# Row-max placings moved from GpSimd's DMA queue to SyncE's, with held-back stack fills and new transfer costs in the planner of an attention and FFN kernel

## Chip, cores and metric

The kernel runs on one core of one Trainium2 chip. The metric is the device time of one execution in microseconds (us), lower is better. Before the change it is 1095.73 us, the median of 3 runs (1094.55 to 1102.3).

## What is computed

One transformer block over x of shape 2 x 1024 x 512, all in float32. With xn the layer norm of x:

```
qkv  = xn @ w_qkv.T + b_qkv                    # 32 heads of 16
s    = softmax(q k.T / 4 + alibi, causal) v    # per head
s    = s @ w_out.T + b_out
h    = silu(oct(xn, w_gate)) * oct(xn, w_up)   # 1360 hidden; the weights cut to -1, 0, 1
out  = x + s * silu(oct(h, w_down))
```

`oct` is a linear map whose weight matrix is put together from eight blocks by the multiplication table of the octonions. The softmax is the exact one: the row maximum is subtracted before the exponential.

## The kernel before

**Attention in units.** Heads are worked on in groups of four, in units `(b, g, qc)`: batch `b`, head group `g` (8 of them), half `qc` of the 1024 queries. There are 32 units. Each needs these pieces:

- *Projections* (`qk_items`, L460): q and k of a pair of head groups, in float32. ScalarE and VectorE put the result into a tile `st` as a rounded high part and the remainder, and one transfer of 512 KB on SyncE's queue (L495) sends it to a scratch `sp` in DRAM. The weights of the next pair (`wqr`) are fetched on SyncE's queue (L486) and compacted by GpSimd (`compact_wq`, L151).
- *Stack fills* (`fill_k`, L513, and `fill_q`, L526): the parts are read back from `sp` into stacks `k_stack` (a ring of five) and `q_stack` (a ring of four), four transfers of 128 KB for each, and a fifth of 16 KB with the alibi rows for a k stack. A fill overwrites a stack that an earlier group used, so it waits for TensorE to be done with that one.
- *Maxima* (`max_items`, L537): first score products (L552), `s1` in the program, whose rows VectorE reduces to their maxima (`left`, `mx`). `split_max` (L601) splits the maxima into two float32r parts.
- *Placing* (`place_max`, L611): four transposes on TensorE (L617, tile `pm`), a copy by ScalarE to `mr` (L624), and two transfers of 8 KB (L625 to L628) that put the two parts into rows 126 and 127 of the unit's q stack. They are issued on GpSimd's queue. With these rows the second score product subtracts the row maximum by itself.
- *Exponentials* (`exp_step`, L657): second score products (L668, `s2`), a mask product (L687) on the diagonal, and the exponential by ScalarE from one of two PSUM banks into a tile `p`.
- *Values* (`value_step`, L694): p times v (L706), and `normalise` (L719), whose result goes to a DRAM scratch `att`.

Beside them run side items: v products (L434), the projections of later pairs, the output projection (L775, tiles `ot`, `y`, scratch `proj`), and the preparation of the FFN's weights (three sums `tot_g`, `tot_u`, `tot_d`, and sign expansions that leave through `mw` on GpSimd's queue). After the last unit comes the FFN (L1415 and L1444), in a fixed order.

**What sets the order.** Each engine takes its instructions in the order in which the program wrote them, and SyncE's and GpSimd's queues do so too: a transfer whose wait is not over holds up all that stand behind it. That order is made at build time by a small planner in the kernel (L1097 to L1358). It keeps a clock of TensorE (`now`), and assumed times at which ScalarE, VectorE, PSUM banks and transfers will be done, and always emits the item that is ready first, with priorities. `link` stands for the transfers. An item that needs a placing counts as ready at `placed[u]`, which is 6000 ns after the copy to `mr` (L1207); a fill takes the link for 4500 ns and is there 2500 ns later (L1133, L1134); fetched and stored tiles are there after 6000 and 5000 ns (L1142, L1219); a projection's parts after 4000 ns (L1276). A fill is emitted in `try_fill` (L1122) as soon as its stack is no longer needed by an item still to be emitted. None of these numbers is in the program that runs: there, an instruction waits for the real event, but in the order that the planner chose.

The planner's numbers touch only the stage before the FFN. SyncE's queue has eight completion semaphores in rotation, so its transfers wait in turn for the one eight places before them.

Of the kernel before, what the change touches and what calls it, by code (L numbers as in the profile page):

```python
# [75 lines left out]
def kernel(  # L76
# [21 lines left out]
    act_, dve_, pool_, sp_ = (  # L98
        InOrder(tc, engine, held) for engine in (nc.scalar, nc.vector, nc.gpsimd, nc.sync)
    )  # L100
# [3 lines left out]
    def pe(ins):  # L104

        return tc.keep_in_program_order(ins)
# [301 lines left out]
    def q_of(b, g, half):  # L408
        return q_ring[(2 * (b * NG + g) + half) % 4]
# [201 lines left out]
    def place_max(b, g, qc, tiles):  # L611

        q = q_of(b, g, qc)
        ps = ps_m.tile([P, 512], F32, tag="m", name=f"pm_{b}_{g}_{qc}")
        for tl in range(4):
            pe(
                nc.tensor.transpose(  # L617
                    ps[0:8, tl * P : (tl + 1) * P],
                    tiles["rm"][:, tl].rearrange("p l h -> p (l h)"),
                    ident,  # L620
                )
            )
        mr = wk.tile([8, 512], F32R, tag="mr", name=f"mr_{b}_{g}_{qc}", bufs=1)
        act_.copy(mr, ps[0:8, :])  # L624
        for n in range(2):  # L625
            pool_.dma_start(
                out=q[NR - 2 + n : NR - 1 + n].bitcast(F32),
                in_=mr[4 * n : 4 * n + 4, :].bitcast(F32),  # L628
            )
# [89 lines left out]
    def normalise(b, g, qc):  # L719

        posb = po_tiles.pop((b, g, qc))
        o = op.tile([P, 4, 64], F32, tag="o", name=f"o_{b}_{g}_{qc}")
        pt = ps_m.tile([P, 4, 4, 32], F32, tag="m", name=f"pt_{b}_{g}_{qc}")
        for tl in range(4):
            pe(
                nc.tensor.transpose(
                    pt[:, tl, :, :].rearrange("p h e -> p (h e)"),
                    posb[:, tl * P : (tl + 1) * P],
                    ident,
                )  # L730
            )
        rl = wk.tile([P, 4, 4, 1], F32, tag="rl", name=f"rl_{b}_{g}_{qc}")
        dve_.reciprocal(rl, pt[:, :, :, HD : HD + 1])
        dve_.tensor_tensor(
            o.rearrange("p t (h d) -> p t h d", d=HD),
            pt[:, :, :, 0:HD],
            rl.to_broadcast([P, 4, 4, HD]),
            ALU.mult,
        )
        n = b * (S // P) + 4 * qc  # L740
        sp_.dma_start(
            out=att[n : n + 4, :, g * 64 : (g + 1) * 64].rearrange("t p n -> p t n"), in_=o
        )
# [67 lines left out]
    units = [(b, g, qc) for b in range(B) for g in range(NG) for qc in range(2)]  # L811
# [9 lines left out]
    maxs, mtiles = [], []  # L821
    for u in range(NU):
        its, t = max_items(*units[u])
# [18 lines left out]
    E, V, M = [0], [0], [0]  # L842
    stored = {}
    fills = [0]
    fetches, fetched, last_outs = {}, {}, []
    turned_out = [0]

    def unit_of(lst, n):
        return lst[n][0] if n < len(lst) else NU

    for b in range(B):
        for hh in range(2):
            n = 2 * b + hh
            u = 8 * n
# [10 lines left out]
        for gp in range(2 - 2 * b, NP):  # L865
            n = b * NP + gp
            u = 4 * n
# [6 lines left out]
        for n, qc in enumerate((0, 1) if b + 1 < B else (1, 0)):  # L874
            u = (b + 1) * 2 * NG + n
# [21 lines left out]
    for n in order:  # L897
        if n in seen:
            continue
        k = n  # L900
# [193 lines left out]
    now, kind = [HEAD], ["F"]  # L1094
    act, dve = [0.0], [0.0]
    e_free, x_free, m_free = [0.0] * 2, [0.0] * 3, [0.0] * 2
    o_free = [0.0]  # L1097
    p_ready, placed, fill_at = {}, {}, []
    link = [0.0]
    turns, norms = [], []  # L1100
    S_ = [0]

    def take(pool):
        pool.sort()
        return pool

    def run_pe(k, ready, cost):
        now[0] = max(ready, now[0] + SWITCH.get((kind[0], k), 0)) + cost
        kind[0] = k

    def run_act(t, cost):
        act[0] = max(act[0], t) + cost
        return act[0]

    def run_dve(t, cost):
        dve[0] = max(dve[0], t) + cost
        return dve[0]


    qk_done = [HEAD + 4500]  # L1120

    def try_fill():  # L1122

        n, part = divmod(fills[0], 4)
        if n >= B * NG or len(qk_done) <= (n // 2 + 1 if n > 1 else part // 2):
            return
        if n == 0 and now[0] < qk_done[part // 2] - 4000:
            return
        if unit_of(exps, E[0]) < 2 * (n - 2) + (0, 1, 2, 2)[part]:
            return  # L1130
        (fill_q if part % 2 else fill_k)(n // NG, n % NG, part // 2)
        fills[0] += 1
        link[0] = max(now[0], link[0], qk_done[n // 2 + 1 if n > 1 else part // 2]) + (4500 if n else 3000)  # L1133
        fill_at.append(link[0] + 2500)  # L1134

    def try_fetch():
        for n, k in enumerate(fetches):
            if k in fetched or k not in stored or stored[k] > now[0]:
                continue
            if turned_out[0] == 4 * n:  # L1140
                fetches[k]()
                fetched[k] = now[0] + 6000  # L1142

# [51 lines left out]
    def next_turn():  # L1197
        found = []
        if turns:
            u, t = turns[0]  # L1200

            def go(u=u):
                turns.pop(0)
                place_max(*units[u], mtiles[u])
                run_pe("F", ready, 436)
                take(m_free)[0] = run_act(now[0] + START, 500)
                placed[u] = m_free[0] + 6000  # L1207

            ready = max(t, min(m_free))
            found.append((ready, 1, 0, go))  # L1210
        if norms:
            u, t = norms[0]

            def go(u=u):
                norms.pop(0)
                normalise(*units[u])
                run_pe("F", t2, 436)
                take(m_free)[0] = run_dve(now[0] + START, 600)
                stored[units[u]] = m_free[0] + 5000  # L1219

            t2 = max(t, min(m_free))
            found.append((t2, 2, 0, go))
        return [f for f in found if f[0] < HELD]
# [27 lines left out]
    def next_side(pos):  # L1251
        if S_[0] == len(side):
            return []
        due, ok, (cost, emit, what, *need) = side[S_[0]]
        if not ok():
            return []

        def go():
            emit()
            S_[0] += 1  # L1260
            if cost:
                run_pe("F", ready, cost)
            if what == "none":
                return
            if HELD not in m_free:
                take(m_free)[0] = HELD
            if what is None:
                return
            if what == "v":
                end = run_dve(now[0] + START, 350)  # L1270
            elif what == "qk":
                end = run_dve(run_act(now[0] + START, 600), 700)
                done_qk[0] += 1

                if done_qk[0] % 4 == 0:
                    qk_done.append(end + 4000)  # L1276
            elif what == "t":
                end = run_act(now[0] + START, 500)
            else:
                end = run_dve(now[0] + START, 600)  # L1280
            m_free[m_free.index(HELD)] = end + END

        ready = 0 if HELD in m_free or not cost else min(m_free)
        for k in need:
            ready = max(ready, known[k] + 100)
        return [(ready, 3 if pos >= due else 7, cost, go)]

    def next_behind(pos):
# [62 lines left out]
    while E[0] < len(exps) or V[0] < len(vals) or S_[0] < len(side) or norms or behind:  # L1351
        try_fill()
        try_fetch()
        if not w_again and unit_of(exps, E[0]) >= NU - 5:
            fetch_signs()
        if not step():
            now[0] += 500
            assert now[0] < 1e8  # L1358
# [5 lines left out]
    for t in [  # L1364
# [9 lines left out]
        t = t.rearrange("p h n -> p (h n)")[:, 0 : 12 * P]  # L1374
# [138 lines left out]
    for n, (tb, mt) in enumerate(work):  # L1513
# [10 lines left out]
        if n >= 1 and last_outs:  # L1524
            while True:
                _, emit, kind = last_outs.pop(0)
# [77 lines left out]
```

## Time and profile before

| What | Value |
|---|---|
| median of 3 runs | 1095.73 us (1094.55 to 1102.3) |
| the profiled execution | 1096.36 us, its span 1094.6 us |
| TensorE busy | 1043.3 us (95%) |
| VectorE, ScalarE, GpSimd busy | 676.4, 509.7, 174.4 us |
| transfers on SyncE's queue, and GpSimd's | 98.28 MB, 4.77 MB |
| placings' transfers | 64 of 8 KB, median 2.5 us from issue to landing |
| fills' transfers | 128 of 128 KB for the k stacks, 4.9 us; 128 for the q stacks, 4.4 us |

In the profile PE is TensorE's matmuls, PEld its weight loads, DVE VectorE, ACT ScalarE, POOL GpSimd, SP SyncE; a q behind the name means the engine's queue or sequencer. Tiles are named without their numbers: `q_stack<-mr` is a placing's transfer, `q_stack<-sp` a fill's. All instructions that go through the helper at L69 show that line, so they are told apart by their tiles. Busy shares of PE are of modelled matmul times and overlap a little: a 128x512 product in a row of its like follows the one before by about 0.23 us although each is shown as longer. A float32 product is two instructions in the trace.

### The profile page before, as it was taken

The numbers are of one execution on the slowest core, as the hardware profiler recorded it, in microseconds if no ns is written. First come the engines' busy times: TensorE is split into PE (matmuls) and PEld (weight loads), VectorE is DVE, ScalarE is ACT, GpSimd is POOL, SyncE is SP. The second block draws the span as 40 slices with busy tenths as digits, with TensorE's granted clock in tenths as the row PEclk, the third lists the DMA queues.
The fourth block names the chain that finished last, engine by engine and source line by source line (L and its number), as shares of the span: only waits on it lengthen the run. The fifth ranks groups of instructions, "written<-read, shape, count | busy, mean of one in ns | idle before, by whom it ended". The sixth has DMA issues, their size and how long they took to land. (4 is left out here: it accounts for less than half of the span.)

```text
span 1094.6 us, 15494 instructions
## 1 busy us (share of the span) xinstructions
PE 1043.3 (95%) x5578; PEld 701.0 (64%) x5578; DVE 676.4 (62%) x1405; ACT 509.7 (47%) x958; POOL 174.4 (16%) x290
## 2 busy tenths in 40 slices
PE   9858998999999999999999999999899999999995
PEld 6535565676656566666576665666456678888784
DVE  5358798678878876787887778868432123141312
ACT  3103457675666544555554555566581213232322
POOL 4710003201010011010101000000011123232322
PEclk9979998999999999999999999999999999999998
DMA  5794574445366444384544235841141123030211
GB/s 161 180 162 128 129 141 135 93 83 108 70 165 104 95 107 55 102 165 83 144 71 65 64 65 122 159 84 45 44 131 49 49 58 116 1 116 1 77 39 38
DMA packets 73195, 104.04 MB, mean 95 GB/s; under 512 B 25896, under 2 KB 30640, under 8 KB 73120
## 3 DMA queue, kind: packets, MB, share of 16 engines
q1 hardware_dynamic: 69648, 98.28, 39.5%
q0 software_dynamic: 3472, 4.77, 1.7%
q8 instruction: 45, 0.74, 0.3%
q14 instruction: 30, 0.25, 0.1%
HBM read 69.39 MB, written 33.10 MB: 94 GB/s over the span
## 5 line engine op out<-in xcount | busy, mean ns | idle before, releaser
L69 ACT ACTIVATE p<-s 128x512 f32<-128x512 f32 x576 | 318.6, 595 | 188.6 <-PE s L687 113.0
L668 PE MATMUL s<-q_stack,k_stack 128*128 128x512 f32 (+3 forms) x768 | 255.0, 399 | 4.7 <-ACT p L69 4.3
L552 PE MATMUL s<-k_stack,q_stack 126*128 126x512 f32 (+3 forms) x768 | 238.3, 390 | 7.9 <-DVE mx L69 6.5
L69 DVE TENSOR_REDUCE mx<-s 128x1 f32<-128x384 f32 (+3 forms) x352 | 226.2, 643 | 11.5
L69 DVE TENSOR_REDUCE left<-s 128x1 f32<-128x512 f32 x256 | 164.0, 683 | 38.3 <-PE s L552 37.2
L668 PEld LDWEIGHTS s<-q_stack,k_stack 128*128 128x128 f32 x768 | 134.0, 190 | 74.3 <-ACT p L69 36.1
L552 PEld LDWEIGHTS s<-k_stack,q_stack 126*128 126x128 f32 x768 | 129.2, 191 | 64.2 <-issue 18.4
L69 DVE TENSOR_TENSOR s<-s,mask 128x128 f32<-128x128 f32 (+2 forms) x352 | 123.8, 352 | 47.0 <-PE s L552 46.5
L706 PE MATMUL po<-p,v 128*32 128x512 f32 (+3 forms) x1536 | 140.5, 491 | 0.4 <-ACT p L69 0.4
L476 PE MATMUL pqk<-xnT,wq 128*128 128x512 f32 x256 | 135.5, 629 | 5.0 <-POOL wq L69 4.0
L69 DVE SCALAR_TENSOR_TENSOR h<-pu,sc_u,sg 128x512 f32<-128x512 f32 (+1 forms) x44 | 33.0, 750 | 157.0 <-PE pu L1423 153.7
L69 POOL DMA_DIRECT2D q_stack<-mr x64 | 32.0, 505 | 580.6 <-ACT mr L69 580.6
L69 POOL TENSOR_TENSOR hs<-h,hs 128x512 fp32r<-128x512 f32 (+1 forms) x43 | 56.2, 1306 | 213.0 <-ACT hs L69 213.0
L706 PEld LDWEIGHTS po<-p,v 128*32 128x32 f32 x1536 | 42.8, 109 | 72.9 <-issue 66.1
L687 PE MATMUL s<-mask_r,ident_r 128*128 128x256 f32 (+1 forms) x320 | 89.0, 278 | 0.0
L69 ACT ACTIVATE sg<-pg,sc_g 128x512 f32<-128x512 f32 (+1 forms) x44 | 30.3, 688 | 99.9 <-PE pg L1423 99.8
L476 PEld LDWEIGHTS pqk<-xnT,wq 128*128 128x128 f32 x256 | 47.5, 201 | 31.6 <-issue 21.1
L69 ACT CAST hs<-h 128x512 fp32r<-128x512 f32 (+1 forms) x44 | 27.3, 619 | 85.6 <-DVE h L69 85.6
L434 PE MATMUL pv<-wv,xnT 128*128 128x256 f32 x256 | 66.3, 386 | 0.6 <-ACT md L69 0.6
L687 PEld LDWEIGHTS s<-mask_r,ident_r 128*128 128x128 f32 x320 | 60.5, 189 | 3.1 <-issue 2.2
L775 PE MATMUL pout<-wo_sb,oT 128*128 128x512 f32 x128 | 61.8, 598 | 0.5 <-ACT oT L69 0.5
L434 PEld LDWEIGHTS pv<-wv,xnT 128*128 128x128 f32 x256 | 46.1, 190 | 13.0 <-issue 6.5
(146 smaller groups left out, 1088.9 us busy)
## 6 DMA issues: line engine op xcount, KB each, us to landing
sp<-st SPq DMA_DIRECT2D x32, 512.0 KB, 3.4
k_stack<-sp SPq DMA_DIRECT2D x128, 128.0 KB, 4.9
q_stack<-sp SPq DMA_DIRECT2D x128, 128.0 KB, 4.4
wqr<-in_wqk_dram SPq DMA_DIRECT2D x16, 512.0 KB, 5.2
xt<-in_x_dram SPq DMA_DIRECT2D x16, 256.0 KB, 3.5
att<-o SPq DMA_DIRECT2D x32, 128.0 KB, 3.6
ot<-att SPq DMA_DIRECT2D x16, 256.0 KB, 3.4
proj<-y SPq DMA_DIRECT2D x16, 256.0 KB, 2.0
```

The lines of the kernel that those rows point to most:

```text
L69: ins = issue(*args, **kwargs)
L434: nc.tensor.matmul(ps[:, 0:256], lhsT=xnT[:, c, b * S + kt * P : b * S + (kt + 1) * P], rhs=wv_tiles[2 * b + hh][:, c, :], start=(c == 0), ...
L476: nc.tensor.matmul(ps, lhsT=wq_tiles[b, gp][:, kt, which, :], rhs=xnT[:, kt, b * S + c * 512 : b * S + (c + 1) * 512], start=(kt == 0), st ...
L552: nc.tensor.matmul(ps[:, j * n : (j + 1) * n], lhsT=q_of(b, g, qc)[0 : NR - 2, first + j, tl * P : (tl + 1) * P], rhs=k_of(b, g, c)[0 : NR ...
L668: nc.tensor.matmul(ps[:, c0 : c0 + w], lhsT=k_of(b, g, kt // 4)[0:NR, h, kt % 4 * P : (kt % 4 + 1) * P], rhs=q[0:NR, h, 512 - w : 512], st ...
L687: pe(nc.tensor.matmul(out, lhsT=ident_r, rhs=rhs, start=False, stop=True))
L706: nc.tensor.matmul(po[32 * i : 32 * i + 32, 512 - w : 512], lhsT=v[:, kt, h * VC : h * VC + 32], rhs=p[:, i * part + c0 : i * part + c0 + ...
L775: nc.tensor.matmul(ps, lhsT=turned[t][:, c, :], rhs=wo_sb[0][:, c, :], start=(c == 0), stop=(c == KD - 1),)
```

## The change

Three things are changed, and nothing else. The two transfers of a placing are issued on SyncE's queue instead of GpSimd's. `try_fill` emits no fill while a placing is near, which is when a finished unit's maxima wait for their transposes, when at most five items of a unit's maxima are left, or when a placing has been emitted and its assumed time is not over; the test is left out where the next maxima need just that fill, and for the first group. And every transfer now takes its share of the one `link`: 3400 ns for a k fill and 2700 for a q fill, 1400 for a fetch, 100 for a placing, 700 for a store, 2700 for a projection's parts, each there about 2000 ns later. A placing so counts as there some 2500 ns after its copy instead of 6000. The amount of work on every computing engine stays the same; its order changes in the stage before the FFN.

```diff
@@ place_max
         for n in range(2):
-            pool_.dma_start(
+            sp_.dma_start(
                 out=q[NR - 2 + n : NR - 1 + n].bitcast(F32),
                 in_=mr[4 * n : 4 * n + 4, :].bitcast(F32),
             )
@@ planner
+    def transfer(t, cost):
+
+        link[0] = max(link[0], t) + cost
+        return link[0]
+
+    def placing_soon():
+
+        if M[0] == len(maxs):
+            return False
+        u, n, count, *_ = maxs[M[0]]
+        if fills[0] <= 4 * (u // 2) + 1 + 2 * units[u][2]:
+            return False
+        return bool(turns) or count - n <= 5 or any(p > now[0] for p in placed.values())
+
     def try_fill():
...
+        if n and placing_soon():
+            return
         if unit_of(exps, E[0]) < 2 * (n - 2) + (0, 1, 2, 2)[part]:
             return
         (fill_q if part % 2 else fill_k)(n // NG, n % NG, part // 2)
         fills[0] += 1
-        link[0] = max(now[0], link[0], qk_done[n // 2 + 1 if n > 1 else part // 2]) + (4500 if n else 3000)
-        fill_at.append(link[0] + 2500)
+        start = max(now[0], qk_done[n // 2 + 1 if n > 1 else part // 2])
+        fill_at.append(transfer(start, 2700 if part % 2 else 3400) + 2300)
@@ try_fetch
-                fetched[k] = now[0] + 6000
+                fetched[k] = transfer(now[0], 1400) + 2300
@@ next_turn, after place_max
-                placed[u] = m_free[0] + 6000
+                placed[u] = max(m_free[0] + 600, transfer(m_free[0], 100)) + 1900
@@ next_turn, after normalise
-                stored[units[u]] = m_free[0] + 5000
+                stored[units[u]] = transfer(m_free[0], 700) + 2300
@@ next_side, after the last projection of a pair
-                    qk_done.append(end + 4000)
+                    qk_done.append(transfer(end, 2700) + 2000)
```

## The prediction

> **What bounds the kernel now.** I read the page's slices first, then the stages, the waits, and one tight unit. The slices show TensorE busy nearly everywhere, with the granted clock down in two places:
>
> ```profile
> PE   9858998999999999999999999999899999999995
> PEclk9979998999999999999999999999999999999998
> ```
>
> The busy times by stage (columns: length, then busy us of PE, PEld, DVE, ACT, POOL, granted clock, DMA share, GB/s) say where TensorE is idle:
>
> ```profile
> 50.00:100.00 50.00, 35.98 (x169) 23.39 (x168) 33.10 (x65) 9.53 (x16) 7.58 (x69) 0.86 0.75 132
> 100.00:150.00 50.00, 47.15 (x223) 27.21 (x222) 42.66 (x87) 21.63 (x39) 3.99 (x12) 0.97 0.64 144
> 150.00:200.00 50.00, 42.91 (x224) 25.76 (x223) 43.33 (x90) 31.17 (x77) 12.95 (x20) 0.90 0.55 141
> 200.00:750.00 550.00, 546.11 (x3350) 353.04 (x3351) 429.83 (x920) 314.60 (x570) 44.29 (x97) 1.00 0.48 99
> 750.00:808.00 58.00, 52.76 (x315) 30.25 (x313) 33.78 (x106) 39.95 (x94) 1.99 (x4) 0.97 0.22 63
> ```
>
> From 200 to 750 us, where 24 of the 32 placings are, TensorE is idle for 3.9 us of 550. From 50 to 200 it is idle for 24 us, 12.6 of them one wait for weights. The waits of the whole span (who waited <- for what: us in total, times, longest):
>
> ```profile
> POOL q_stack L69 <- ACT mr L69: 580.6, 31, 39.8
> PEld s L668 <- ACT p L69: 36.1, 129, 1.5
> DVE wsum_g L69 <- DMA w_g<-in_wg_dram: 12.9, 1, 12.9
> PE tot_g L329 <- DVE wsum_g L69: 12.6, 1, 12.6
> ```
>
> No wait for a placing is among them. GpSimd's queue sat 581 us waiting to issue one, at no cost to itself. How a tight unit goes, (1,1,1), shows in the timeline (start, length):
>
> ```profile
> 519.19 0.60 PE L617 MATMUL pm<-ident,rm 128*8 128x128 f32 x4
> ...
> 519.83 0.57 ACT L69 CAST mr<-pm 8x512 fp32r<-8x512 f32 x1 [1.70 <-PE pm L617]
> ...
> 520.69 0.99 POOL L69 DMA_DIRECT2D q_stack<-mr  x2 [28.76 <-ACT mr L69]
> ...
> 524.48 1.02 PE L476 MATMUL pqk<-xnT,wq 128*128 128x512 f32 x2
> 524.94 1.24 PE L552 MATMUL s<-k_stack,q_stack 126*128 126x512 f32 x2
> ...
> 527.57 1.03 PE L668 MATMUL s<-q_stack,k_stack 128*128 128x512 f32 x2
> ```
>
> The transposes start at 519.19, the copy ends at 520.41, and the transfers land at 524.24 and 525.66. Their first user starts at 527.57, 1.9 us later, and TensorE works all the while. So the old plan's 6 us were paid with other work, not with idle time. Over all 32 units the trace has the second landing before the first use, by 0.6 to 35.5 us. What bounds the stage is TensorE's own work, and making placings quick saves nothing by itself. A gain can come only from a better order.
>
> **The change, part by part.**
>
> *Queue.* GpSimd loses 64 issues of 505 ns, 32 us of an engine idle for most of the span. One place gains. A compaction stood behind a placing, and a projection waited for it:
>
> ```profile
> 426.85 1.00 POOL L69 DMA_DIRECT2D q_stack<-mr  x2 [33.13 <-ACT mr L69]
> 427.84 1.93 POOL L69 COPY wq<-wqr 128x128 f32<-128x128 f32 x8
> 429.12 1.13 PE L476 MATMUL pqk<-xnT,wq 128*128 128x512 f32 x2 [1.54 <-POOL wq L69]
> ```
>
> In the built program this pair's compaction stands behind no placing any more: **-1.5 us**. SyncE gets 64 issues; its smallest ones now (16 KB alibi rows) take about 0.3 us, so 19 us in a queue that mostly waits. They cost only where something urgent follows.
>
> *Landing.* On GpSimd's queue, from the end of the copy to the second landing, the quiet units take 2.5 us, and 14 of the 32 take 3.9 to 8.8. On SyncE's, two issues of 0.3 and a landing as of the fastest row there (`proj<-y`, 2.0 us) make 2.4 to 2.6; behind a spill of 512 KB (3.4 us) or a fill (4.4 to 4.9) it would be 5 to 7. I take 2.4 where SyncE's order has nothing large just ahead, else 4.4.
>
> *What the new order leaves between placing and use.* I priced TensorE's instructions between a placing's transposes and the unit's first exponential product, in both built orders, at start-to-start times of the trace (0.23, 0.18, 0.12 and 0.06 us for score products of 512, 384, 256 and 128 columns, 0.86 for a float32 product, 0.86 for four value products). Unit (1,1,1) had 10 maxima products, 4 projection products and a value block, 7.1 us; now 5, 1 and a block, 3.0. Real time is 1.11 of this price (placings (0,3,0) to (1,6,1): 518.6 us for a price of 465.2). Six units now have under 4 us: (0,1,1) 3.5, (0,5,1) and (1,1,1) 3.0, (0,6,1) and (1,2,1) 2.4, (1,7,1) 3.7. Before, one had. Needed are 0.8 us from the transposes' end to the copy's end, and the landing: 3.2 quiet. Times 1.11, (0,6,1) and (1,2,1) lack 0.5 us each. (0,5,1) and (1,1,1) have a 512 KB spill issued just ahead, so they need 5.2 and lack 1.9 each. TensorE takes its work in order, so what is lacking is idle time: **+5 us**. Bounds: 0 (everything lands in 2.4), and 30 (the eight units under 5 us all land 3.7 us later, at 6.2, as late ones did before).
>
> *Fills held back.* Before, at least 10.4 us of priced work lay between the emission of a q fill of the second half and its first use; now (0,3,1) has 2.7, (0,2,1) 5.9, and ten others 6.9 to 9.0. A pair of k and q fills takes 2.1 us to issue the first, 1.7 the second, and 4.4 to land: about 8. A q fill alone takes 4 to 5 from issue to landing. (0,3,1) lacks 1.8, (0,2,1) about 1, the rest together a few tenths: **+3 us**, bounds 0 and 24 (twelve fills 2 us late, one spill of 512 KB beside each).
>
> *Weights of the third projection pair.* In the new SyncE order their load stands behind the store of the first `o`, whose transposes come 4.1 us of work before the first user; the old order had a wait of 2.45 us there. Load (5.2), half a compaction (1.5), two issues and VectorE make over 8: **+2 us**, bounds 0 and 4.5.
>
> *Order of the exponentials.* With two PSUM banks, back-to-back exponentials make TensorE wait for ScalarE: 36.1 us in all, 23.0 of it in 200 to 750. The new order has 156 pairs of banks in a row instead of 204, so up to a quarter of that goes; the runs of value products rise from 78 to 85, at about 0.2 us a change. **-4 us**, bounds -8 and 0.
>
> *First weights.* `w_g` stands at the same place of SyncE's order, behind the same transfers, so it lands as late; the new order does one score product more before that wait (0.2 us, left out). If its cover went, the 12.6 us would grow.
>
> The sum is -1.5 + 5 + 3 + 2 - 4 = +4.5 us on the profiled execution's 1096.4, which is 0.6 above the median of the runs: 1101 us, +0.4%.
>
> **A rule of the notes against the row.** The trace shows placings landing 1.7 to 8.0 us after issue, median 2.5, beside a SyncE queue that carried 98 MB. The Trainium skill, DMA: Bandwidth & Descriptors, section Queues, rings and completion order, says that each DMA engine goes round robin between the queue rows that have work, and takes one row's descriptors in ring order. By that, GpSimd's queue let the small placings pass between SyncE's large ones, and on SyncE's own queue they wait behind them: every tight unit with a transfer in flight would pay for it, and the sum would be nearer its upper bound. The same page, section Latency and other measured facts, gives a first byte after about 0.6 us for SyncE's kind of queue and 1 for GpSimd's; by that figure, as an estimate, (0,6,1) and (1,2,1) would lack almost nothing. No row of this profile separates the two.
>
> **Rivals.** (1) *Slower: the head of SyncE's queue.* A placing lands behind the spills, loads and fills that the hold does not cover, at the tight units from (0,5,1) on and at (1,6,1), where two fills stand 4 us ahead. For it: 14 of the 32 placings before took 3.9 us or more even on a queue of their own. Against: the hold keeps fills away. It decides from about 1.5 us more at each of eight units, 12 us on top: 1113. (2) *Faster: the plan fits.* Landings are as assumed, so 5, 3 and 2 become about 0, and the start gains: half of the 11 idle us from 50 to 200 that are not the first weights, and the clock of 0.86 and 0.90 rising with it, say 3 us. Together 1096.4 - 5.5 - 6 - 3 = 1082. Against: the start hangs on weights and on ScalarE, not on placings. (3) *It cancels*: 1101, the forecast.
>
> **How the numbers follow.** Within 1% of before (1084.8 to 1106.7; about what a measurement here tells from no change) 0.52, the forecast's case; slower by more 0.33, rival 1; faster by more 0.15, rival 2. The range takes in rival 1 with half of the upper bounds' excess (1122), and ends 4 us short of rival 2: 1086 to 1122. The forecast's own range is 1090 to 1107.
>
> **What would show it.** Right: in the new profile, waits of exponential products for `q_stack<-mr` at (0,5,1), (0,6,1), (1,1,1), (1,2,1) of 0.5 to 2 us, waits of maxima products for q fills at (0,2,1) and (0,3,1), no wait for the compaction at the fifth batch of weights, fewer waits on `p`. Wrong: idle TensorE time from 50 to 200 us changing by over 6 us, or placings at a median over 4 us.

## The result, and the profile after

The changed kernel takes 1128.98 us (median of 4 runs, 1124.33 to 1131.94), the kernel before 1096.86 beside it: a ratio of 1.0274, 95% interval 1.0253 to 1.0295. It is slower by 32 us. Forecast were 1101 us, a loss of 4.5, and a range up to 1122: the direction was right, the size far too small. The profiled execution took 1131.94 us, its span is 1130.2, against 1094.6 before.

The slices of the new page, with the DMA row under them:

```profile
PE   9858888899999999988999999999989999999997
PEclk9879897999999999998999999999999999999999
DMA  5794167333662831734291246375122123011021
```

and the DMA row of the page before:

```profile
DMA  5794574445366444384544235841141123030211
```

From the fourth slice to the twenty-sixth, DMA was rather even before, mostly 3 to 6 tenths; now it swings between 1 and 9. Transfers are held, then let go together. The stages of the changed kernel (length, then busy us of PE, PEld, DVE, ACT, POOL, granted clock, DMA share, GB/s):

```profile
50.00:100.00 50.00, 35.91 (x160) 22.87 (x159) 32.95 (x65) 9.00 (x15) 5.92 (x67) 0.86 0.82 142
100.00:150.00 50.00, 43.19 (x174) 24.09 (x172) 37.55 (x75) 17.41 (x31) 2.02 (x8) 0.90 0.34 94
150.00:200.00 50.00, 41.03 (x231) 25.66 (x229) 36.21 (x75) 29.22 (x69) 7.38 (x11) 0.86 0.68 155
200.00:787.00 587.00, 563.93 (x3399) 358.32 (x3398) 440.40 (x942) 324.86 (x588) 23.06 (x52) 0.99 0.47 95
787.00:846.00 59.00, 54.20 (x317) 30.79 (x317) 35.53 (x103) 38.30 (x90) 0.00 (x0) 0.97 0.18 54
```

TensorE is now idle for 23 us in the long stretch, where it was for 3.9; from 50 to 200 it is idle for 30 instead of 24. The last value product of the attention starts at 846.2 us instead of 806.4: 39.8 us are lost ahead of the FFN. What follows it is 4.2 us shorter than before, of which more below. The waits that answer to those shown of before, with three new ones:

```profile
PEld s L668 <- ACT p L69: 29.6, 95, 1.6
DVE wsum_g L69 <- DMA w_g<-in_wg_dram: 14.1, 1, 14.1
PE tot_g L329 <- DVE wsum_g L69: 13.6, 1, 13.6
PE pqk L476 <- POOL wq L69: 11.3, 2, 8.3
PE s L552 <- DMA q_stack<-sp: 3.1, 3, 1.2
PE s L668 <- DMA q_stack<-mr: 1.7, 2, 1.5
```

Placings are hardly waited for: 1.7 us. Unit (1,1,1), which the forecast thought 1.9 us short, goes like this:

```profile
551.69 0.60 PE L617 MATMUL pm<-ident,rm 128*8 128x128 f32 x4
...
552.33 0.58 ACT L69 CAST mr<-pm 8x512 fp32r<-8x512 f32 x1 [1.70 <-PE pm L617]
...
552.91 0.38 SPq L69 DMA_DIRECT2D sp<-st  x1
...
553.38 1.22 SPq L69 DMA_DIRECT2D q_stack<-mr  x2
...
556.27 0.70 PE L668 MATMUL s<-q_stack,k_stack 128*128 128x512 f32 x2 [0.17 <-DMA q_stack<-mr]
```

The copy ends at 552.91, a spill of 512 KB is issued just ahead of the placing, and still the first product waits 0.17 us. The fifth batch of weights has lost its wait for a compaction, as forecast:

```profile
446.08 1.08 PE L434 MATMUL pv<-wv,xnT 128*128 128x256 f32 x4
446.99 1.88 PE L476 MATMUL pqk<-xnT,wq 128*128 128x512 f32 x4
```

The largest new wait is that of the next batch, pair (1,2):

```profile
497.44 0.57 ACT L69 CAST mr<-pm 8x512 fp32r<-8x512 f32 x1 [0.70 <-PE pm L617]
...
498.05 1.21 SPq L69 DMA_DIRECT2D q_stack<-mr  x2
...
499.35 1.79 SPq L69 DMA_DIRECT2D k_stack<-sp  x4
501.19 0.29 SPq L69 DMA_DIRECT2D k_stack<-al_dram  x1
501.58 1.71 SPq L69 DMA_DIRECT2D q_stack<-sp  x4
503.48 1.29 SPq L69 DMA_DIRECT2D wqr<-in_wqk_dram  x2
...
510.60 1.01 POOL L69 COPY wq<-wqr 128x128 f32<-128x128 f32 x4 [115.36 <-DMA wqr<-in_wqk_dram]
...
512.13 2.07 PE L476 MATMUL pqk<-xnT,wq 128*128 128x512 f32 x2 [8.27 <-POOL wq L69]
```

SyncE's last issue ahead of this was the store of an `o` at 493.02. At the head of SyncE's queue then stood the placing, until the copy ended at 498.01; behind it the k and q fills of (1,1,1), which had been held back; behind them the weights, issued at 503.48. Without the hold the same load is issued at 487.82 and the wait is 0.62 us:

```profile
486.52 1.21 SPq L69 DMA_DIRECT2D q_stack<-mr  x2
487.82 0.86 SPq L69 DMA_DIRECT2D wqr<-in_wqk_dram  x2
...
491.46 2.15 POOL L69 COPY wq<-wqr 128x128 f32<-128x128 f32 x8 [80.71 <-PE s L687]
...
492.95 1.12 PE L476 MATMUL pqk<-xnT,wq 128*128 128x512 f32 x2 [0.62 <-POOL wq L69]
```

### The profile page after: what moved, and what is told of

It is laid out like the page before. It is cut to its first block, busy times and chain, and to the rows that moved or that the text cites. A ratio compares the mean times of both kernels' runs of the same rounds, so it can differ in the third digit from the quotient of the medians.

```text
span 1130.2 us, 15451 instructions
## 1 busy us (share of the span) xinstructions
PE 1057.7 (94%) x5578; PEld 702.9 (62%) x5578; DVE 677.8 (60%) x1405; ACT 512.8 (45%) x958; POOL 142.7 (13%) x226
## 3 DMA queue, kind: packets, MB, share of 16 engines
q0 software_dynamic: 1424, 4.24, 1.2%
## 5 line engine op out<-in xcount | busy, mean ns | idle before, releaser
L69 ACT ACTIVATE p<-s 128x512 f32<-128x512 f32 x576 | 322.8, 596 | 205.6 <-PE s L687 117.2
L552 PE MATMUL s<-k_stack,q_stack 126*128 126x512 f32 (+3 forms) x768 | 245.9, 396 | 19.1 <-DVE mx L69 12.9
L476 PE MATMUL pqk<-xnT,wq 128*128 128x512 f32 x256 | 139.1, 647 | 14.4 <-POOL wq L69 11.3
L706 PE MATMUL po<-p,v 128*32 128x512 f32 (+3 forms) x1536 | 145.2, 499 | 0.4 <-ACT p L69 0.4
L434 PE MATMUL pv<-wv,xnT 128*128 128x256 f32 x256 | 68.7, 386 | 0.0
L69 POOL COPY wq<-wqr 128x128 f32<-128x128 f32 x64 | 15.9, 294 | 407.0 <-DMA wqr<-in_wqk_dram 341.9
L69 ACT ACTIVATE st<-pqk,bqk_sb 128x512 fp32r<-128x512 f32 x32 | 21.9, 688 | 70.0 <-PE pqk L476 58.8
```

The costliest lines, as they stand in the source:

```text
L69: ins = issue(*args, **kwargs)
L434: nc.tensor.matmul(ps[:, 0:256], lhsT=xnT[:, c, b * S + kt * P : b * S + (kt + 1) * P], rhs=wv_tiles[2 * b + hh][:, c, :], start=(c == 0), ...
L476: nc.tensor.matmul(ps, lhsT=wq_tiles[b, gp][:, kt, which, :], rhs=xnT[:, kt, b * S + c * 512 : b * S + (c + 1) * 512], start=(kt == 0), st ...
L552: nc.tensor.matmul(ps[:, j * n : (j + 1) * n], lhsT=q_of(b, g, qc)[0 : NR - 2, first + j, tl * P : (tl + 1) * P], rhs=k_of(b, g, c)[0 : NR ...
L706: nc.tensor.matmul(po[32 * i : 32 * i + 32, 512 - w : 512], lhsT=v[:, kt, h * VC : h * VC + 32], rhs=p[:, i * part + c0 : i * part + c0 + ...
```

## Experiments: which of the three parts

Theory one: the queue. A placing at the head of SyncE's queue waits for a copy, so that SyncE can't run ahead of TensorE (it stood 73.8 us behind copies) and all behind it is late. Theory two: the hold. Fills come late, and the order around them is worse. Each part was taken away or left alone.

**q_only**, the queue's move alone, all engines' order that of before:

```diff
 (kernel before)
-            pool_.dma_start(
+            sp_.dma_start(
```

> The kernel before with one edit: the two transfers of each placing are issued by SyncE's queue. The planner is the old one, so every engine's order of work is that of before but for the 64 issues. Queue theory: a placing at the head of SyncE's queue waits for ScalarE's copy, so SyncE can't run ahead of TensorE and the loads, spills and fills behind it go out late (in the changed kernel SyncE stood 73.8 us behind copies, and the weights of one projection pair came 8.4 us late behind one placing). Then this kernel takes half of the 32 us or more: 1112 to 1128 us, with a stall at projections' first products. Hold theory: the loss is in the new order, because held fills land late (1.2 to 2.1 us each at five units, some 12 us at 169 to 228 us) and the clock falls with the stalls. Then this one is within 6 us of before: 1092 to 1103.

**plan_only**, hold and reckoning, placings on GpSimd's queue:

```diff
 (changed kernel)
-            sp_.dma_start(
+            pool_.dma_start(
```

> The changed kernel with one edit: the placings are issued by GpSimd's queue again, the new planner's order (hold and reckoning) is kept. Queue theory: the stall of 8.4 us at 512 us and most of the rest go, 1098 to 1108 us. Hold theory: it stays at 1118 to 1130, with the waits for q fills and the idle TensorE from 169 to 228 us as in the changed kernel.

**no_hold**, queue and reckoning:

```diff
 (changed kernel)
-        if n and placing_soon():
-            return
```

> The changed kernel without the test that holds fills back; placings on SyncE's queue, transfers reckoned by their share. Fills now stand between placings and the head of the queue. Queue theory: as slow as the changed kernel or slower, 1120 to 1140 us, with exponential products waiting 2 us and more for placings behind fills. Hold theory: 1095 to 1106 us, waits for q fills gone.

**reckon_only**, both edits of plan_only and no_hold, so that the reckoning alone is left:

> The reckoning of transfers alone: placings on GpSimd's queue, no hold. TensorE's order is that of the kernel without the hold. Both theories: near the kernel before, 1092 to 1104 us. A third reading, that the shorter reckoned landings alone make the order too tight (units (1,1,1) with 3.0, (1,5,1) 5.0, (1,6,1) 2.8 us of priced work between placing and first use), would give 1106 us or more.

Medians in us, ratio to before with its interval:

| order of the work | placings on GpSimd | placings on SyncE |
|---|---|---|
| old | before, about 1097.6 | q_only 1098.78: 1.0009 (0.9992 to 1.0026) |
| reckoned | reckon_only 1110.58: 1.0125 (1.0095 to 1.0154) | no_hold 1102.56: 1.0051 (1.0032 to 1.0070) |
| reckoned, with the hold | plan_only 1141.52: 1.0400 (1.0379 to 1.0420) | changed 1128.98: 1.0274 (1.0253 to 1.0295) |

The queue theory falls: placings on SyncE's queue cost nothing that shows with the old order, and with both new orders they save 8 and 12.5 us. The hold costs 31 us with placings on GpSimd's queue, and plan_only lies 11 us above the range that the theory of the hold gave it; on SyncE's queue the hold costs 26. The reckoning costs 13 and 4. reckon_only lies in the range of its third reading, an order too tight for placings, but its products wait for placings for 2.1 us only, so that cause is not shown. In the order with the hold, products wait for placings far longer on GpSimd's queue than on SyncE's, where it was 1.7 us; of plan_only:

```profile
PE s L668 <- DMA q_stack<-mr: 10.9, 5, 4.7
```

In the reckoned order these waits are 2.1 us on GpSimd's queue and 1.2 on SyncE's, and in the old order none on GpSimd's and 1.6 on SyncE's. So which queue serves placings better hangs on the order here.

The Trainium skill, DMA: Bandwidth & Descriptors, section Queues, rings and completion order, says that an engine goes round robin between queue rows, by which one would expect a queue of their own to serve placings sooner. The old order agrees (none against 1.6 us), the order with the hold does not (10.9 against 1.7), and there the measurement decides. The same page's section Latency and other measured facts gives SyncE's kind of queue the shorter first byte, which has the sign of the two new orders and not of the old one. What made the placings of plan_only late stays open.

## Experiments: what of the hold

**hold_late**, the hold from the fills of (0,4) on:

```diff
-        if n and placing_soon():
+        if n > 3 and placing_soon():
```

> The changed kernel, with the hold in force only from the fills of (0,4) on; the early fills of (0,2) and (0,3) go out as without the hold. Lateness theory (held fills go out only when their own maxima are next, and are late throughout; min 7 us of priced work between emission and first use at eight q fills here, as in the changed kernel): the changed kernel lay 6.7 to 9.8 us behind the one without the hold at (0,1,0) to (0,3,1), that goes, the later 22 stay: 1117 to 1124 us. Start theory (the fills of (0,2), moved by 20 us of work, starve the maxima at 140 to 230 us, the granted clock falls to 0.86 and 0.90 and the rest only follows): 1102 to 1110.

**hold_inflight**, one condition of three:

```diff
-        return bool(turns) or count - n <= 5 or any(p > now[0] for p in placed.values())
+        return any(p > now[0] for p in placed.values())
```

> The changed kernel, with one of the hold's three conditions: a fill is held only while a placing that was issued has not landed by the plan. The q fills of second halves have the leads of the kernel without the hold (8 to 20 us of priced work, one 5.2), those of first halves 12 to 27. Lateness theory: 1099 to 1107. If any hold costs, by fills bunched ahead of other transfers whenever it lets go: 1112 or more.

**hold_ahead**, the other two:

```diff
-        return bool(turns) or count - n <= 5 or any(p > now[0] for p in placed.values())
+        return bool(turns) or count - n <= 5
```

> The changed kernel, with the other two of the hold's conditions: fills are held while a placing waits for its transposes or five or fewer groups of maxima lie ahead of it. Leads of second-half q fills 6 to 13 us of priced work, one 2.7, against 7 to 9 with the whole hold. Lateness theory: between the two, 1108 to 1120. Bunching theory: as the changed kernel, 1122 to 1132.

**hold_2**, the reach of the second condition shortened:

```diff
-        return bool(turns) or count - n <= 5 or any(p > now[0] for p in placed.values())
+        return bool(turns) or count - n <= 2 or any(p > now[0] for p in placed.values())
```

> The changed kernel with two groups of maxima instead of five as the reach of the hold. Lateness theory: the loss grows with the reach; leads of second-half q fills are 8 to 20 us of priced work, one 5.5, so 1104 to 1112. Any-hold theory (a fill held for a placing always lands on the critical path): 1118 or more.

**hold_lead**, the two fills that follow the one needed set free:

```diff
-        if fills[0] <= 4 * (u // 2) + 1 + 2 * units[u][2]:
+        if fills[0] <= 4 * (u // 2) + 3 + 2 * units[u][2]:
```

> The changed kernel, in which a fill is no longer held once it is one of the two that follow the fill of the unit whose maxima are being taken (the test compares with 4 * (u // 2) + 3 instead of + 1): the fills for the next unit are free, all three conditions hold the others. Leads of second-half q fills 8.7 to 15 us, one 5.5. Lateness theory: the loss of the hold (26 us) goes but for a few us, 1099 to 1108. If the loss lies in the conditions' effect on the rest of the order and not in the fills' lead: 1115 or more.

| kernel | us | ratio to before |
|---|---|---|
| hold_late | 1132.08 | 1.0313 (1.0287 to 1.0339) |
| hold_inflight | 1102.08 | 1.0038 (1.0025 to 1.0052) |
| hold_ahead | 1123.59 | 1.0236 (1.0205 to 1.0267) |
| hold_2 | 1110.26 | 1.0109 (1.0090 to 1.0127) |
| hold_lead | 1114.99 | 1.0162 (1.0131 to 1.0193) |

The early fills are not it: without their hold the time is no better (1132, which is 8 us above the range of the lateness theory too), and the start theory falls. Holding only while a placing is under way costs nothing against no_hold. The cost is in the look ahead, and it grows with its reach. hold_ahead came out 4 us above what the lateness theory gave it, and hold_lead 7 above, where its rival began, though its fills had leads like no_hold's. So the lead of fills was not the whole; the stall at 512 us (8.7 in hold_ahead, 8.3 in hold_late, 2.8 in hold_lead) pointed to what stands behind them.

**after_early**, the changed kernel with the next pair's weights loaded from the middle of a pair on:

```diff
-            if (which, c, kt) == (1, 1, KD - 1) and n < B * NP:
+            if (which, c, kt) == ((1, 1, KD - 1) if n == 1 else (1, 0, 0)) and n < B * NP:
                 load_wq((n // NP, n % NP), sp_)
```

> The changed kernel, with the load of each next pair's projection weights issued at the middle of the pair before (product (1,0,0)) instead of at its last product. In the changed kernel TensorE waits 8.4 us for these weights at 512 us and 3.2 at 112; a load behind held fills and placings. If the hold's cost lies partly in what is queued behind held fills: those two waits go but for a compaction (1.5 us each), 1118 to 1122 us. If the stall only stands in for another one (the q fills and placings are as late, and TensorE waits there instead): 1126 to 1130.

**nh_early**, the same edit in no_hold:

> The changed kernel without the hold and with the early load of projection weights; it stands against the same kernel with the hold, 1117.06 us. Of the waits for weights the kernel without the hold has 3.2 us: 1098 to 1101 us, so that the hold's cost without the weights is 16 to 19 us. If early weights bring as much here as with the hold (11.6), the weights' stall was not the hold's doing: 1090 to 1093.

**hold_half**, after_early with first halves' fills held only:

```diff
-        if n and placing_soon():
+        if n and part < 2 and placing_soon():
```

> The changed kernel with early projection weights, in which only fills of first halves are held. Fills of second halves now have 8.2 us and more of priced work ahead of their use, one 5.5. If the rest of the hold's cost is the late second-half fills (waits of 1.6 to 2.0 us at 376, 460, 553 and 637 us, and what they drag along): 1100 to 1108 us. If it is the reordering of the early maxima: 1112 to 1118.

after_early takes 1117.06 us (1.0166, 1.0146 to 1.0187), nh_early 1097.03 (1.0002, 0.9988 to 1.0015), hold_half 1094.66 (0.9985, 0.9966 to 1.0004). Early weights give 11.9 us back with the hold and 5.5 without it: more than expected of either. The rest of the hold's cost is 20 us, and all of it goes when only the fills of second halves are free, which ends 5 us below the range that was expected. What these fills do in the changed kernel shows at (1,2,1):

```profile
560.30 1.86 SPq L69 DMA_DIRECT2D k_stack<-sp  x4
562.21 0.29 SPq L69 DMA_DIRECT2D k_stack<-al_dram  x1
562.60 3.20 SPq L69 DMA_DIRECT2D q_stack<-sp  x4
...
568.56 0.63 PE L668 MATMUL s<-q_stack,k_stack 128*128 128x512 f32 x1
570.35 0.93 PE L552 MATMUL s<-k_stack,q_stack 126*128 126x512 f32 x3 [1.16 <-DMA q_stack<-sp]
```

The fill is emitted 9.0 us of priced work ahead of this product and issued 7.8 us ahead of it; the last of its four transfers starts near 565, and 5 us later TensorE still waits. In hold_half no wait for a q fill is left. That wait line is only 3.1 us in all, though. Of the 29.9 us between the spans of the changed kernel and no_hold, 18.3 are idle TensorE (72.5 against 54.2) and 11.6 longer busy time of the same 5578 instructions (1057.7 against 1046.1). The granted clock is 0.90 and 0.86 from 100 to 150 and 150 to 200 us, where no_hold has 0.97, and 0.95 from 500 to 600, where no_hold has 1.00; how much of the 11.6 us this makes is not shown.

The traces of after_early and nh_early say what the 20 us are not. Waits of maxima products, first of after_early, then of nh_early:

```profile
PE s L552 <- DVE mx L69: 15.4, 21, 3.1
PE s L552 <- DMA q_stack<-sp: 3.0, 3, 1.3
```

```profile
PE s L552 <- DVE mx L69: 7.1, 15, 2.2
PE s L552 <- DMA q_stack<-sp: 3.0, 1, 3.0
```

TensorE waits for q fills for 3.0 us in both. Of the 21.0 us between their spans 12.0 are idle TensorE (63.1 against 51.1) and 9.0 longer busy time, and the largest item of the idle time is that products wait 8.3 us longer for VectorE's maxima. The held fills move the maxima products, so that the order may bring them where VectorE is not ready. That is not the whole either, since hold_half has 11.1 us of these waits and loses nothing. So it is shown that freeing the fills of second halves removes the loss. That also changes the order of all engines, so it is not shown that their late landing is the loss, nor how the 20 us divide between waits, clock and order.

## Experiments: the queue by itself

**split**, the kernel before with row 0 of each placing on SyncE's queue and row 1 on GpSimd's:

```diff
 (kernel before)
-            pool_.dma_start(
+            (sp_, pool_)[n].dma_start(
```

> The kernel before with one of each placing's two transfers on SyncE's queue and one on GpSimd's. GpSimd's last step was 8.71 us with 3472 packets in its queue and 3.49 with 1424. If it goes by their number, 2448 packets make 6.1 us, and the program's end comes some 2.6 us earlier than before's after the last product. If it goes by whether placings use that queue at all, 8.7.

The program ends with a drain of each engine. GpSimd's, the longest of the three times on each line (min, median, max in ns), in before, split and q_only:

```profile
L1600 POOLq DRAIN  x3: 46/98/8715, 1085.1 to 1094.3; - x3
```

```profile
L1600 POOLq DRAIN  x3: 46/98/6096, 1092.1 to 1098.7; - x3
```

```profile
L1600 POOLq DRAIN  x3: 46/98/3486, 1092.0 to 1097.0; - x3
```

and the packets of GpSimd's queue in before, split and q_only:

```profile
q0 software_dynamic: 3472, 4.77, 1.7%
```

```profile
q0 software_dynamic: 2448, 4.50, 1.6%
```

```profile
q0 software_dynamic: 1424, 4.24, 1.5%
```

Each 1024 packets fewer make the drain about 2.6 us shorter, 2.55 ns a packet. The drain is nearly in proportion to the packets (2.51, 2.49 and 2.45 ns for each), and not to the placings on the queue, of which q_only has none. From the last FFN product's start to the end are 12.06, 9.45 and 7.88 us. So 4.2 us of the queue's move are gained at the very end, and within the attention q_only loses 6.9 (its last value product starts at 813.3, against 806.4); in the sum they nearly cancel. The gain is in the other orders too: from the last value product to the end, the changed kernel takes 4.1 us less than plan_only, and no_hold 3.3 less than reckon_only, of 9.8 and 9.5 us between their spans. split took 1100.81 us in its one run.

**q_early**, q_only with the early weights:

```diff
 (q_only)
-            if (which, c, kt) == (1, 1, KD - 1) and n < B * NP:
+            if (which, c, kt) == ((1, 1, KD - 1) if n == 1 else (1, 0, 0)) and n < B * NP:
```

> The old planner with placings on SyncE's queue (which alone measured 1.0009 of before, with 8.3 us of waits for projection weights), and the weights' load issued at the middle of the pair before. If those waits were what the queue's move cost within the stage: 1089 to 1094 us, first below before. If the early load of 1 MB pushes fills and spills out instead: 1096 to 1102.

1089.94 us, 0.9924 (0.9908 to 0.9940): faster than both kernels. q_only waited 8.3 us for projection weights where the kernel before waited 4.0, so 4.3 of its loss of 6.9 within the attention were these waits; the wait for `w_g` was 1.7 us longer and one placing was waited for 1.6. In q_early no product waits for these weights, and the last value product starts 9.2 us earlier than in q_only. Early weights with placings on GpSimd's queue were not run, so how much of the gain over the kernel before needs the move of the queue is not shown.

**q_early_g**, with the ternary weights reckoned later:

```diff
 (q_early)
-            lambda: set_known(("l", name), now[0] + 9000),
+            lambda: set_known(("l", name), now[0] + 22000),
```

> As the kernel before it with placings on SyncE and early projection weights, and the planner told that w_g, w_u and w_d land 22 us after their issue is emitted instead of 9, so that the product that waits for the sum of w_g stands 12 us of work later. If the 12 to 14 us for which TensorE waits there is a wait for a late load with other work at hand: 1080 to 1088. If the work put ahead of it only waits elsewhere (the early stretch has no other work that is ready): 1090 to 1096.

1105.37 us, 1.0061 (1.0042 to 1.0080): neither range. The wait for `w_g` is gone, and a placing took its place; a second placing is waited for 6.5 us at 122 us:

```profile
70.00 2.25 SPq L69 DMA_DIRECT2D w_g<-in_wg_dram  x3
...
72.71 0.40 SPq L69 DMA_DIRECT2D wv<-in_wv_dram  x1
73.50 2.35 SPq L69 DMA_DIRECT2D w_u<-in_wu_dram  x3
76.38 1.62 SPq L69 DMA_DIRECT2D q_stack<-mr  x2
...
85.98 0.76 PE L668 MATMUL s<-q_stack,k_stack 128*128 128x512 f32 x1 [12.86 <-DMA q_stack<-mr]
```

**q_early_g2** puts the placings of (0,0) back:

```diff
 (q_early_g)
-            sp_.dma_start(
+            (sp_ if (b, g) > (0, 0) else pool_).dma_start(
```

> The kernel of 1105.37 us with the product that waits for w_g moved 12 us back, in which TensorE waited 13.4 us at 86 us for the first unit's placing, issued on SyncE's queue behind w_g and a backlog of fills; here the placings of (0,0) alone go to GpSimd's queue. If the head of SyncE's queue is that wait: 1083 to 1093 us, the wait gone. If the copies or the transfers themselves are what is late there: 1100 to 1106.

1090.34 us, 0.9943 (0.9926 to 0.9959): both waits are gone, with 1.1 us left for placings. Here SyncE's queue, behind a backlog, delayed a placing as rival 1 had it: in q_early_g the copy ended at 66.29, the placing was issued at 76.38, and the product could start at 85.98. In q_early the placing was issued as late, at 77.26, but its product comes after the `w_g` wait, at 88.13, and does not wait for it. Yet q_early_g2 is no faster than q_early: it is 12.0 us ahead of it at the last value product of (0,1,1) and 0.8 at that of (0,2,1). From 150 to 300 us its TensorE is idle for 14.0 us, q_early's for 7.4; what takes the rest back stays open.

## Why the forecast was wrong

*The step that failed* is the term for the fills held back, +3 us with bounds 0 and 24. Measured are 26 us on SyncE's queue and 31 on GpSimd's, above its upper bound. It counted each late fill by itself: emission to use, less the time to issue and land, so that (0,3,1) and (0,2,1) lacked 1.8 and 1. Of such waits the changed kernel has 3.1 us, almost the 3 of the term, but by luck: they are at (0,6,1), (1,0,1) and (1,2,1), and none is at the two units that were named. What the term left out is all that a held fill does beyond its own wait. What stands behind it in SyncE's order is late too: 11.9 us came back with early weights in the changed kernel, 5.5 without the hold, so about 6.4 of the 26 are the weights. And freeing the fills of the second halves removed 20 us more, though waits for q fills are 3.0 us with the hold and without it once the weights are early. How these 20 us come about stays open, as said above.

*Landing*, +5 (0 to 30): 1.7 us of waits. Of the four units named, (1,1,1) waited 0.17 us, with a spill just ahead, and no wait is listed at the others. (0,6,1) and (1,2,1) had 3.3 us from the end of the copy to the first use, where the price of the work left 1.9, so the leads were priced too short. On GpSimd's queue the same order waits 10.9 us.

*Queue*, -1.5: the compaction's wait at the fifth batch went, as forecast, and a wait of 8.3 us came at the sixth (4.1 with placings on GpSimd's queue in plan_only, 0.6 without the hold). "They cost only where something urgent follows" was right, and the urgent thing, the projection weights, was not looked for. The gain at the end of GpSimd's queue, 4.2 us, was not in the sum at all.

*Weights of the third pair*, +2 (0 to 4.5): the two waits for `wq` were 4.0 us with a longest of 2.5, and are 11.3 with a longest of 8.3; the third pair's is 3.0, so +0.5.

*Order of the exponentials*, -4 (-8 to 0): weight loads waited 36.1 us for `p` and wait 29.6, so -6.5. Right in sign; that TensorE's time fell by as much can't be seen under the rest.

*First weights*, left out: 12.6 us became 13.6.

*The reckoning's order* was priced only between placings and their first uses. It costs 13 us with GpSimd's queue and 4 with SyncE's. no_hold is 15.6 us behind the kernel before at the last value product of (0,3,0) and 8.8 at that of the last unit; 3.5 us of it are one wait for the q fill of (0,3,1), which has 5.2 us of work ahead of its use. The rest of this loss stays open.

*The rivals.* Rival 1 had a price of 12 us for placings that land behind other transfers, some 1.5 at each of eight units. At one unit that it named, (1,6,1), the changed kernel shows just that: a k and a q fill are issued from 765.42 to 769.50, the placing at 770.81, and its product waits.

```profile
776.66 0.47 PE L668 MATMUL s<-q_stack,k_stack 128*128 128x512 f32 x1 [1.55 <-DMA q_stack<-mr]
```

But this and the 0.17 us at (1,1,1) are all, so rival 1's mechanism is 1.7 us of the 32. Of "what would show it", the wait of (1,1,1) was 0.17 us where 0.5 to 2 were named, the waits for q fills came at other units, and the compaction's wait and part of those on `p` went, as named. Idle TensorE from 50 to 200 grew by 5.9 us (24.0 to 29.9), just under the 6 that were named as wrong. The median landing can't be read, since the new page gives no landing times for placings on SyncE's queue.

*The range.* Its upper end of 1122 does not come out of the terms: their upper bounds exceed them by 25, 21, 2.5 and 4 us, half of which is 26, so 1127. The measured 1129 lies above both.

## What to carry to other kernels

Before a transfer is held back for another's sake, look at what waits for it and at what is queued behind it in the same order: the hold protected waits of 1.2 us (no_hold's for placings) and cost 26. A load with a free buffer belongs early in an in-order queue, since early weights gained 5.5, 8.8 and 11.9 us in three orders; with them and the old order, placings on SyncE's queue came out 8 us below the kernel before. A change that consists of parts is best measured in all its combinations, because its parts here cost 1, 4 and 26 us in one order of adding them and 13, 31 and -12.5 in another.

## What was not expected of the hardware

GpSimd's drain at the program's end goes by the packets that its queue carried: 8.71, 6.10 and 3.49 us for 3472, 2448 and 1424, in one profiled execution each. The longest drains of the other engines stay as they are in all three (3.2 us on TensorE, 1.7 on VectorE, 0.8 on ScalarE, 7 ns on SyncE). The Trainium skill, VectorE: DVE Perf Modes, section The DRAIN you can't avoid, tells of drains of some 12 ns on all engines, from the code that the runtime puts around a kernel. Each engine but GpSimd has a drain of 7 to 19 ns here, near that figure; the long ones at the program's end are not of that size, GpSimd's least of all.
